# Cross-attention projections through the heads instead of through folded weights, with TensorE in program order

## The chip, the core and the metric

The kernel runs on one core of one Trainium2 chip. The metric is device time in microseconds (us), lower is better. Each engine has its own in-order queue: TensorE (PE, with its weight loads shown as PEld), VectorE (DVE), ScalarE (ACT), GpSimd (POOL), and SyncE (SP), which here only issues transfers. All data are float32.

## The reference

One transformer block on 64 sequences of 32 tokens, width 256. Every sequence has its own context of 257 rows, width 128.

```python
x = x + xattn(layernorm(x), ctx)     # 16 heads of 64: q from x, k and v from ctx (width 128), softmax over 257
x = x + attn(layernorm(x))           # 4 heads of 64 within the 32 tokens, rotary on half of each head
x = x + ffn(layernorm(x))            # 8 experts, top 2 of softmax, silu(a) * b, weighted sum
# xattn:
qh, kh, vh = heads(q @ Wq), heads(kv @ Wk), heads(kv @ Wv)
out = merge(softmax(qh @ kh.T * 64 ** -0.5) @ vh) @ Wo + bo
```

## The kernel before

Keys and values of the cross-attention are never formed. Because the score of head h is `x Wq[h] Wk[h]^T ctx^T`, a setup stage (line 144) multiplies `Wq[h] Wk[h]^T` into `w_qk` (256 x 128 for each head), and likewise `Wv[h] Wo[h]` into `w_vo` (line 158, 128 x 256 for each head). The 257th context row, which does not fit in two blocks of 128, gets a table `u_last` (line 169) that goes to DRAM and comes back by tile (`load_last`). The setup's tiles lie in a pool `raw` that is closed afterwards; a small pool `rope` for the rotary tables comes next.

Tokens are worked in 16 tiles `t` of 128 tokens, that is 4 sequences `b` each. Each (t, b) is one step of the main loop:

- `cross_probs` (L371 to L386): four score matmuls `s` (128 x 257, 32 tokens of 4 heads in the 128 rows). For each, DVE takes the maximum (`nmx`), ACT the exponential and its row sum; then DVE scales all four by the reciprocal sums (`inv`, L380 and L382). It runs one step ahead of its use.
- `probs_transposed` (L394): eight PE transposes `tp` into two banks, copied out to `pt`.
- `cross_mix` (L409): probabilities times context, `pa` (128 x 512), copied by DVE to `cT`.

Two generators fill the loop. `cross_queries(c)` (variable `ahead`) makes the queries of two tiles: layer norm (`normed`, L311 to L319: bn_stats, bn_aggr, a sum on DVE, a power on POOL, a scaling on DVE), transposes `trq`, and for each head two matmuls `pq` (L352) with 256 columns whose results DVE and ACT copy into `q`. `rest(t)` (variable `behind`) does everything that follows for the tile before: `cross_output` (L419, 16 heads into `po`, plus L426 for the last row), then `self_attention` (`trs`, `pqkv`, rotary on DVE, `trqk`, scores `pss`, softmax on DVE and ACT, `pot`, `apo`), then `route` (`trr`, router logits `pr`, running counts `pk`, `pw`, `pb`, and indirect writes of the rows to their expert). The loop takes one piece of each generator at three places of every step. In the attention part only SP's queue keeps the program's order; a scheduler orders PE, DVE, ACT and POOL by readiness in its own model. The pool `ps` gives PSUM banks under the tags `s` (3), `t` (3) and `a` (2).

After the last tile the routed rows go through the experts in 39 blocks (L739 to L790), with PE in program order.

Of the kernel before, what the change touches and what calls it, by code (L numbers as in the profile page):

```python
# [9 lines left out]
FP = mybir.dt.float32  # L10
# [6 lines left out]
P = 128  # L17
# [29 lines left out]
def block_kernel(  # L47
# [6 lines left out]
    xwq_t: bass.AP,  # L54
    xwk_t: bass.AP,
    xwv_t: bass.AP,
# [18 lines left out]
    ctx.enter_context(tc.manual_schedule(engines={SP}))  # L75
    const = ctx.enter_context(tc.tile_pool(name="const", bufs=1))
    ps = ctx.enter_context(tc.tile_pool(name="ps", bufs=3, space=PSUM))

    copies = [0]

    def evacuate(dst, src):
        copies[0] += 1
        if copies[0] % 2:
            nc.vector.tensor_copy(dst, src)
        else:
            nc.scalar.copy(dst, src)  # L86
# [21 lines left out]
    w_qk = const.tile([P, XH, 2, KVD], FP, name="w_qk")  # L108
    w_vo = const.tile([P, XH, D], FP, name="w_vo")
# [11 lines left out]
    setup = ExitStack()  # L121
    raw = setup.enter_context(tc.tile_pool(name="raw", bufs=1))
    xwq_sb = raw.tile([P, XH // 2, D], FP, name="xwq_sb")
    xwk_sb = raw.tile([P, XH // 2, KVD], FP, name="xwk_sb")
    xwv_sb = raw.tile([P, XH // 2, KVD], FP, name="xwv_sb")
    xwo_sb = raw.tile([P, XH // 2, D], FP, name="xwo_sb")
    load(xwq_sb, xwq_t.rearrange("(c p) k -> p c k", p=P))
    load(xwk_sb, xwk_t.rearrange("(c p) k -> p c k", p=P))
    for t in range(2):
        load(xs[t], x[t * P : (t + 1) * P, :])  # L130
    load(xwv_sb, xwv_t.rearrange("(c p) k -> p c k", p=P))
    load(xwo_sb, xwo.rearrange("(c p) k -> p c k", p=P))
    context0 = load_context(0)
    last_sb = const.tile([P, NB], FP, name="last_sb")
    load(last_sb, ctx_last)
    load(xbo_bc, xbo.partition_broadcast(P))

    for h in range(XH):  # L140
        c, r = h // 2, (h % 2) * HD
        pq = ps.tile([P, 2, KVD], FP, tag="s", name=f"pq{h}")
        for k in range(2):
            nc.tensor.matmul(
                pq[:, k, :],
                xwq_sb[r : r + HD, c, k * P : (k + 1) * P],
                xwk_sb[r : r + HD, c, :],
                start=True,
                stop=True,
            )  # L150
        if h % 2:
            nc.vector.tensor_scalar_mul(w_qk[:, h, :, :], pq, QK_SCALE)
        else:
            nc.scalar.mul(w_qk[:, h, :, :], pq, QK_SCALE)
    for h in range(XH):
        c, r = h // 2, (h % 2) * HD
        pv = ps.tile([P, D], FP, tag="t", name=f"pv{h}")
        nc.tensor.matmul(
            pv, xwv_sb[r : r + HD, c, :], xwo_sb[r : r + HD, c, :], start=True, stop=True
        )  # L160
        evacuate(w_vo[:, h, :], pv)


    u_last = tc.dram_tile([4, NB * 4, D], FP, name="u_last")
    u_sb = raw.tile([P, XH // 2, D], FP, name="u_sb")
    for c in range(XH // 2):
        pu = ps.tile([P, D], FP, tag="t", name=f"pu{c}")
        for r in range(2):
            nc.tensor.matmul(
                pu[r * NB : (r + 1) * NB, :], last_sb, w_vo[:, 2 * c + r, :],  # L170
                start=True, stop=True,
            )
        evacuate(u_sb[:, c, :], pu)
    for h4 in range(4):
        r = h4 % 2 * NB
        load(
            u_last[h4].rearrange("(s g) d -> s g d", g=4),
            u_sb[r : r + NB, :, :].rearrange("p (g i) d -> p g i d", i=2)[:, :, h4 // 2, :],
        )
    setup.close()  # L180
# [120 lines left out]
    with attn:  # L301
        qp = attn.enter_context(tc.tile_pool(name="q", bufs=3))
        pp = attn.enter_context(tc.tile_pool(name="p", bufs=3))
        ptp = attn.enter_context(tc.tile_pool(name="pt", bufs=2))
        wk = attn.enter_context(tc.tile_pool(name="wk", bufs=2))
        sm = attn.enter_context(tc.tile_pool(name="sm", bufs=4))

# [14 lines left out]
        def transposed(dst, src, n, name):  # L322

            pt = ps.tile([P, n, P], FP, tag="t", name=f"tr{name}")
            for k in range(n):
                nc.tensor.transpose(pt[:, k, :], src[:, k * P : (k + 1) * P], ident)  # L326
            evacuate(dst, pt)
# [10 lines left out]
        def cross_queries(c):  # L338

            xqT = wk.tile([P, 2, 2 * P], FP, tag="xqT", name=f"xqT{c}")  # L340
            for j in range(2):
                t = 2 * c + j
                xn = normed(t, "q")
                transposed(xqT[:, :, j * P : (j + 1) * P], xn, 2, f"q{t}")
            qs = [qp.tile([P, 4, XH, SEQ], FP, tag="q", name=f"q{2 * c + j}") for j in range(2)]
            for j in range(2):
                queries[2 * c + j] = qs[j]
            yield
            for h in range(XH):
                pq = ps.tile([P, 2 * P], FP, tag="a", bufs=2, name=f"pq{c}_{h}")  # L350
                for k in range(2):
                    nc.tensor.matmul(  # L352
                        pq, w_qk[:, h, k, :], xqT[:, k, :], start=(k == 0), stop=(k == 1)
                    )
                for j in range(2):
                    evacuate(
                        qs[j][:, :, h, :],
                        pq[:, j * P : (j + 1) * P].rearrange("p (b n) -> p b n", n=SEQ),
                    )
                if h % 2:  # L360
                    yield

        def cross_probs(t, b, kvT):


            qb = queries[t][:, b, :, :].rearrange("p h n -> p (h n)")
            sums = sm.tile([P, 4], FP, tag="sums", name=f"sums{t}_{b}")
            pr = pp.tile([P, 4, M], FP, tag="pr", name=f"pr{t}_{b}")
            for g in range(4):
                s = ps.tile([P, M], FP, tag="s", name=f"s{t}_{b}_{g}")  # L370
                nc.tensor.matmul(  # L371
                    s, qb[:, g * P : (g + 1) * P], kvT[:, b, :], start=True, stop=True
                )
                nmx = sm.tile([P, 1], FP, tag="nmx", name=f"nmx{t}_{b}_{g}")
                nc.vector.tensor_reduce(nmx, s, AX.X, ALU.max, negate=True)  # L375
                nc.scalar.activation(  # L376
                    pr[:, g, :], s, AF.Exp, bias=nmx, accum_out=sums[:, g : g + 1]
                )
            inv = sm.tile([P, 4], FP, tag="inv", name=f"inv{t}_{b}")
# [7 lines left out]
            return pr  # L387

        def probs_transposed(t, b, pr, lastT):
            pts = []  # L390
            for j in range(MC):
                tp = ps.tile([P, 4 * P], FP, tag="t", name=f"tp{t}_{b}_{j}")
                for g in range(4):
                    nc.tensor.transpose(  # L394
                        tp[:, g * P : (g + 1) * P], pr[:, g, j * P : (j + 1) * P], ident
                    )
                pt = ptp.tile([P, 4 * P], FP, tag=f"pt{j}", name=f"pt{t}_{b}_{j}")
                if j == 0:
                    nc.vector.tensor_copy(pt, tp)
                else:  # L400
                    nc.scalar.copy(pt, tp)  # L401
                pts.append(pt)
            nc.vector.transpose(lastT[:, b, :], p_last[t % 2][b])
            return pts

        def cross_mix(t, b, pts, kvA, cT):
            pa = ps.tile([P, 4 * P], FP, tag="a", bufs=2, name=f"pa{t}_{b}")
# [6 lines left out]
        def cross_output(t, cT, lastT, ut):  # L414
            xb = wk.tile([P, D], FP, tag="xb", name=f"xb{t}")
            nc.gpsimd.tensor_tensor(xb, xs[t], xbo_bc, ALU.add)
            po = ps.tile([P, D], FP, tag="a", bufs=2, name=f"po{t}")
            for h in range(XH):
                nc.tensor.matmul(  # L419
                    po,  # L420
                    cT[:, h, :, :].rearrange("p b n -> p (b n)"),
                    w_vo[:, h, :],
                    start=(h == 0),
                    stop=False,
                )
            nc.tensor.matmul(  # L426
                po, lastT.rearrange("p b n -> p (b n)"), ut, start=False, stop=True
            )
            nc.vector.tensor_tensor(xs[t], po, xb, ALU.add)

        def self_attention(t):
            xn = normed(t, "s")
# [4 lines left out]
            for lo, hi in ((0, 512), (512, 768)):  # L437
                pq = ps.tile([P, hi - lo], FP, tag="a", bufs=2, name=f"pqkv{t}_{lo}")
# [17 lines left out]
            yield  # L456
            qkT = wk.tile([P, 4, P], FP, tag="qkT", name=f"qkT{t}")
# [6 lines left out]
            for par in range(2):  # L464
                pss = ps.tile([P, 2, SEQ], FP, tag="s", name=f"pss{t}_{par}")
# [30 lines left out]
            pot = ps.tile([P, 2, P], FP, tag="a", bufs=2, name=f"pot{t}")  # L496
# [10 lines left out]
            evacuate(oT, pot)  # L507
# [3 lines left out]
            po = ps.tile([P, D], FP, tag="a", bufs=2, name=f"apo{t}")  # L511
# [4 lines left out]
        def route(t):  # L516


            xr = wk.tile([P, RW], FP, tag="xr", name=f"xr{t}")
            normed(t, "r", xr[:, 0:D])  # L520
# [4 lines left out]
            pr = ps.tile([P, NE], FP, tag="s", name=f"pr{t}")  # L525
# [30 lines left out]
            yield  # L556

            pk = ps.tile([P, NE], FP, tag="s", name=f"pk{t}")
# [17 lines left out]
            pw = ps.tile([NE, P], FP, tag="t", name=f"pw{t}")  # L576
            nc.tensor.transpose(pw, ew, ident)
            ewT = sm.tile([NE, P], FP, tag="rewT", bufs=2, name=f"rewT{t}")
            nc.vector.tensor_copy(ewT, pw)
# [289 lines left out]
```

## Time and profile before

| | |
|---|---|
| three runs | 1050.76 us median (1049.44 to 1054.2) |
| profiled execution | 1047.73 us, span 1046.0 us |
| mean granted TensorE clock in it | 0.946 |
| TensorE busy | 921.9 us, 88% of the span |
| VectorE busy | 582.9 us, 56% |
| ScalarE busy | 304.8 us, 29% |
| first scores; first transposes of probabilities | 53.9 us; 61.2 us |
| `cross_output` of tile 0 begins; of tile 15 begins | 79.5 us; 756.4 us |
| first expert matmul (L763) | 807.2 us |

A line of the profile names the start or the busy time, the engine, the source line, what is written and read, the shape, and in brackets the idle time before it with what ended it. A float32 matmul appears as two instructions (two passes); a transpose as one. An instruction's duration holds its latency, so the rate of a row of matmuls is read from the starts.

### The profile page before, as it was taken

The numbers are of one execution on the slowest core, as the hardware profiler recorded it, in microseconds if no ns is written. First come the engines' busy times: TensorE is split into PE (matmuls) and PEld (weight loads), VectorE is DVE, ScalarE is ACT, GpSimd is POOL, SyncE is SP. The second block draws the span as 40 slices with busy tenths as digits, with TensorE's granted clock in tenths as the row PEclk, the third lists the DMA queues.
The fourth block names the chain that finished last, engine by engine and source line by source line (L and its number), as shares of the span: only waits on it lengthen the run. The fifth ranks groups of instructions, "written<-read, shape, count | busy, mean of one in ns | idle before, by whom it ended". The sixth has DMA issues, their size and how long they took to land. (4 is left out here: it accounts for less than half of the span.)

```text
span 1046.0 us, 15338 instructions
## 1 busy us (share of the span) xinstructions
PE 921.9 (88%) x5272; PEld 713.5 (68%) x5272; DVE 582.9 (56%) x2219; ACT 304.8 (29%) x999; POOL 154.3 (15%) x210
## 2 busy tenths in 40 slices
PE   6599989998999899899989989988863999999992
PEld 5467757675776577577667656756532999999991
DVE  3285775768476666857756685676534333333330
ACT  2262322332232333324223332322200322222220
POOL 3100012011101201100120110011100122222232
PEclk9899998998999999899999999999875999999996
DMA  5600101020101102011110210100003877778722
GB/s 177 201 21 24 39 32 59 1 69 6 54 10 60 59 1 69 6 54 31 39 59 1 69 28 32 54 6 19 16 0 137 283 249 229 233 224 249 207 36 26
DMA packets 39406, 82.82 MB, mean 79 GB/s; under 512 B 5784, under 2 KB 27680, under 8 KB 36256
## 3 DMA queue, kind: packets, MB, share of 16 engines
q1 hardware_dynamic: 32176, 72.38, 20.9%
q0 software_dynamic: 7152, 9.46, 5.0%
q8 instruction: 42, 0.69, 0.3%
q14 instruction: 36, 0.29, 0.1%
HBM read 91.66 MB, written 13.82 MB: 101 GB/s over the span
## 5 line engine op out<-in xcount | busy, mean ns | idle before, releaser
L376 ACT ACTIVATE pr<-s,nmx 128x257 f32<-128x257 f32 x256 | 120.0, 474 | 145.4 <-DVE nmx L375 144.6
L371 PE MATMUL s<-kvT,q 128*128 128x257 f32 x512 | 148.7, 417 | 5.9 <-ACT pr L376 5.1
L352 PE MATMUL pq<-xqT,w_qk 128*128 128x256 f32 x512 | 126.4, 389 | 11.5 <-ACT q L86 11.0
L409 PE MATMUL pa<-pt,kvA 128*128 128x512 f32 x256 | 125.6, 613 | 0.3
L371 PEld LDWEIGHTS s<-kvT,q 128*128 128x128 f32 x512 | 96.4, 203 | 38.2 <-ACT pr L376 14.3
L419 PE MATMUL po<-w_vo,cT 128*128 128x256 f32 x512 | 113.3, 380 | 0.8 <-DVE cT L412 0.8
L352 PEld LDWEIGHTS pq<-xqT,w_qk 128*128 128x128 f32 x512 | 94.0, 193 | 27.4 <-ACT q L86 12.5
L375 DVE TENSOR_REDUCE nmx<-s 128x1 f32<-128x257 f32 x256 | 103.7, 419 | 13.4 <-PE s L371 12.7
L419 PEld LDWEIGHTS po<-w_vo,cT 128*128 128x128 f32 x512 | 97.1, 191 | 15.4 <-DVE cT L412 2.7
L774 DVE SCALAR_TENSOR_TENSOR g<-pb,w1buf,sa 128x128 f32<-128x128 f32 x156 | 44.0, 345 | 107.5 <-PE pb L763 70.0
L790 POOL DMA_INDIRECT out_x<-y,to x39 | 60.6, 1555 | 182.4 <-DMA out_x<-y,to 80.7
L763 PE MATMUL pa<-bxT,w1buf 128*128 128x128 f32 x624 | 77.8, 279 | 4.5 <-DMA w1buf<-in_wall 4.5
L763 PEld LDWEIGHTS pa<-bxT,w1buf 128*128 128x128 f32 x624 | 74.5, 196 | 4.9 <-issue 4.8
L401 ACT COPY pt<-tp 128x512 f32<-128x512 f32 x64 | 37.5, 586 | 136.6 <-PE tp L394 135.1
L763 PE MATMUL pb<-bxT,w1buf 128*128 128x128 f32 x624 | 76.1, 275 | 0.0
L394 PE MATMUL tp<-ident,pr 128*128 128x128 f32 x512 | 75.2, 282 | 0.2
L784 PE MATMUL py<-w2buf,g 128*128 128x256 f32 x312 | 73.8, 380 | 0.8 <-DVE y L789 0.8
L382 DVE TENSOR_SCALAR pr<-pr,inv 128x256 f32<-128x256 f32 x256 | 74.1, 349 | 0.9
L763 PEld LDWEIGHTS pb<-bxT,w1buf 128*128 128x128 f32 x624 | 72.9, 192 | 0.0
L409 PEld LDWEIGHTS pa<-pt,kvA 128*128 128x128 f32 x256 | 45.3, 193 | 40.1 <-issue 23.7
L394 PEld LDWEIGHTS tp<-ident,pr 128*128 128x128 f32 x512 | 62.7, 146 | 9.1 <-issue 3.1
L86 ACT COPY q<-pq 128x128 f32<-128x128 f32 x128 | 33.9, 266 | 103.0 <-PE pq L352 67.1
(196 smaller groups left out, 1085.3 us busy)
## 6 DMA issues: line engine op xcount, KB each, us to landing
w1buf<-in_wall SPq DMA_DIRECT2D x39, 1028.0 KB
w2buf<-in_wall SPq DMA_DIRECT2D x39, 512.0 KB
kvT<-in_ctx_t SPq DMA_DIRECT2D x16, 514.0 KB
kvA<-in_ctx_a SPq DMA_DIRECT2D x16, 512.0 KB
xg<-routed SPq DMA_DIRECT2D x39, 132.5 KB
x<-in_x SPq DMA_DIRECT2D x16, 128.0 KB
out_x<-x SPq DMA_DIRECT2D x16, 128.0 KB
routed<-none SPq DMA_DIRECT2D x8, 132.5 KB
```

Source lines behind the costliest of these rows:

```text
L352: nc.tensor.matmul(pq, w_qk[:, h, k, :], xqT[:, k, :], start=(k == 0), stop=(k == 1))
L371: nc.tensor.matmul(s, qb[:, g * P : (g + 1) * P], kvT[:, b, :], start=True, stop=True)
L375: nc.vector.tensor_reduce(nmx, s, AX.X, ALU.max, negate=True)
L376: nc.scalar.activation(pr[:, g, :], s, AF.Exp, bias=nmx, accum_out=sums[:, g : g + 1])
L382: nc.vector.tensor_scalar(pr[:, g, :ML], pr[:, g, :ML], inv[:, g : g + 1], None, ALU.mult)
L394: nc.tensor.transpose(tp[:, g * P : (g + 1) * P], pr[:, g, j * P : (j + 1) * P], ident)
L409: nc.tensor.matmul(pa, kvA[:, b, j, :], pts[j], start=(j == 0), stop=(j == MC - 1))
L419: nc.tensor.matmul(po, cT[:, h, :, :].rearrange("p b n -> p (b n)"), w_vo[:, h, :], start=(h == 0), stop=False,)
L763: nc.tensor.matmul(dst[:, j, :], w[:, lo : lo + P], xT[:, k, :], start=(k == 0), stop=(k == 1),)
L774: nc.vector.scalar_tensor_tensor(g[:, j, :], pb[:, j, :], w[:, B1 + 4 + j : B1 + 5 + j], sa[:, j, :], ALU.add, ALU.mult,)
L784: nc.tensor.matmul(py, g[:, j, :], w[:, j * D : (j + 1) * D], start=(j == 0), stop=(j == 3),)
L790: nc.gpsimd.indirect_dma_start(out=out[:, :], out_offset=bass.IndirectOffsetOnAxis(ap=to[:, b : b + 1], axis=0), in_=y, in_offset=None, co ...
```

## The change

The folded weights, the setup stage and the pools `raw` go. Queries are made in two steps: `pqh` = x Wq for two heads at a time (K = 128, 128 columns of stationary, 256 moving), scaled by ACT into `qh`; then `of_heads`, which multiplies each head's 64 rows of `qh` with its 64 rows of `Wk`, the even head on rows 0 to 63 of the array and the odd head on rows 64 to 127, into two banks that ACT copies to `q`. The output goes likewise: `pov`, each head's `cT` with 64 columns of `Wv`, even heads to columns 0 to 63 of the array and odd heads to 64 to 127, copied to `ov`, then eight matmuls with `Wo` into `po`. The table of the last row (`last_rows`) is made in the first step of the main loop. TensorE is in program order everywhere. The loop now places single steps: `behind` has six places in each (t, b), the four scores are taken in groups of 2, 1 and 1, and `ahead` starts at an even tile and is spread over two tiles. Empty `yield`s leave places unused. PSUM tags become `s` 3, `t` 2, `a` 3; `p` and `q` pools have two buffers; all `pt` copies and the transposes' copies go to ACT.

```diff
-    ctx.enter_context(tc.manual_schedule(engines={SP}))
+    ctx.enter_context(tc.manual_schedule(engines={SP, mybir.EngineType.PE}))
...
+    for t in range(2):
+        load(xs[t], x[t * P : (t + 1) * P, :])
+    load(xwq_sb, xwq.rearrange("(c p) k -> p c k", p=P))
     load(xwk_sb, xwk_t.rearrange("(c p) k -> p c k", p=P))
+    context0 = load_context(0)
+    load(xwv_sb, xwv)
...
         def cross_queries(c):
             xqT = wk.tile([P, 2, 2 * P], FP, tag="xqT", name=f"xqT{c}")
+            xns = [normed(2 * c + j, "q") for j in range(2)]
+            yield
             for j in range(2):
-                t = 2 * c + j
-                xn = normed(t, "q")
-                transposed(xqT[:, :, j * P : (j + 1) * P], xn, 2, f"q{t}")
...
+                transposed(xqT[:, :, j * P : (j + 1) * P], xns[j], 2, f"q{2 * c + j}")
+            def of_heads(i):
+                pq = [bank([2, 8, SEQ], f"pq{c}_{i}_{par}") for par in range(2)]
+                for mm in range(2):
+                    m = 2 * i + mm
+                    for par in range(2):
+                        r = par * HD
+                        nc.tensor.matmul(
+                            pq[par][:, mm, :, :].rearrange("p b n -> p (b n)"),
+                            xwk_sb[r : r + HD, m, :],
+                            qh[r : r + HD, m, :],
+                            start=True, stop=True,
+                        )
+                for par in range(2):
+                    dst = q[:, :, 4 * i + par : 4 * i + par + 3 : 2, :]
+                    nc.scalar.copy(dst.rearrange("p b h n -> p h b n"), pq[par])
+            for i in range(4):
+                yield
...
+                nc.scalar.mul(qh[:, 2 * i : 2 * i + 2, :], pq, QK_SCALE)
+                if i:
+                    yield
+                    of_heads(i - 1)
+            yield
+            of_heads(3)
...
         def cross_output(t, cT, lastT, ut):
-            for h in range(XH):
-                nc.tensor.matmul(po, cT[:, h, :, :].rearrange("p b n -> p (b n)"), w_vo[:, h, :], start=(h == 0), stop=False)
+            for half in range(2):
+                pv = bank([4, P], f"pov{t}_{half}")
...
+                        nc.tensor.matmul(
+                            pv[par * HD : (par + 1) * HD, i, :],
+                            xwv_sb[:, h * HD : (h + 1) * HD],
+                            cT[:, h, :, :].rearrange("p b n -> p (b n)"),
+                            start=True, stop=True,
+                        )
+                if half:
+                    nc.scalar.copy(ov[:, 4:, :], pv)
+                else:
+                    nc.vector.tensor_copy(ov[:, :4, :], pv)
+                yield
...
             nc.vector.tensor_tensor(xs[t], po, xb, ALU.add)
...
         def rest(t, cT, lastT, ut):
-            cross_output(t, cT, lastT, ut)
-            yield
-            yield from self_attention(t)
-            yield
-            yield from route(t)
+            yield from cross_output(t, cT, lastT, ut)
+            xn = normed(t, "s")
+            yield
+            yield
+            yield from self_attention(t, xn)
+            xr = wk.tile([P, RW], FP, tag="xr", name=f"xr{t}")
+            normed(t, "r", xr[:, 0:D])
+            yield
+            yield
+            yield from route(t, xr)
...
+            probs_transposed(t, b, 0, pr, pts)
             next(behind, None)
+            next(scores, None)
+            next(scores, None)
+            next(behind, None)
+            probs_transposed(t, b, 1, pr, pts)
+            nc.vector.transpose(lastT[:, b, :], p_last[t % 2][b])
+            next(behind, None)
+            next(scores, None)
+            next(behind, None)
+            next(scores, None)
             next(ahead, None)
-            pts = probs_transposed(t, b, now, lastT)
             next(behind, None)
             cross_mix(t, b, pts, kvs[t][1], cT)
             next(behind, None)
-            next(ahead, None)
+            if b % 2 == 0:
+                next(ahead, None)
```

## The prediction

> **What bounds the kernel now.** I read the page's head first.
>
> ```profile
> span 1046.0 us, 15338 instructions
> ...
> PE 921.9 (88%) x5272; PEld 713.5 (68%) x5272; DVE 582.9 (56%) x2219; ACT 304.8 (29%) x999; POOL 154.3 (15%) x210
> ...
> PEclk9899998998999999899999999999875999999996
> ```
>
> TensorE bounds the attention and the experts; only its work and its gaps count. I therefore cut the span by the timeline into A (to 79.5, `cross_output` of tile 0), B (tiles 1 to 15, to 756.4, 676.8 us) and C (the rest, 289.6). The TensorE timeline gives rates from starts.
>
> ```profile
> 24.15 3.67 PE L169 MATMUL pu<-w_vo,last_sb 128*64 128x256 f32 x32
> ...
> 556.03 1.89 PE L352 MATMUL pq<-xqT,w_qk 128*128 128x256 f32 x8
> 557.76 1.04 PE L394 MATMUL tp<-ident,pr 128*128 128x128 f32 x8
> 558.73 0.38 PE L469 MATMUL pss<-qkT 64*32 64x32 f32 x32
> 559.04 1.99 PE L352 MATMUL pq<-xqT,w_qk 128*128 128x256 f32 x8
> ...
> 562.99 0.66 PE L499 MATMUL pot<-diag,qkv 128*64 128x128 f32 x8 [0.15 <-DVE diag L494]
> 563.58 0.70 PE L371 MATMUL s<-kvT,q 128*128 128x257 f32 x2
> ...
> 572.68 0.44 PE L326 MATMUL trr<-ident,xr 128*128 128x128 f32 x2 [0.61 <-DVE xr L319]
> ```
>
> Eight `pq` passes of 256 columns take 557.76 - 556.03 = 1.73 us, 0.216 each; 128 columns cost 0.109. `pu`, on alternating column halves, needs 3.67/32, about 0.11 for 256 columns: halves run two at a time. In the pair of tiles from 495.7 to 585.2 (89.5 us) the passes at these rates make 74.9 us (`po` 14.0, `s` 13.9, `pq` 13.8, `pa` 13.7, `tp` 7.0, the rest 12.5), so 14.6 are gaps. In all of B passes make 550 and gaps 127. About 29 of the gaps (1.9 a tile) belong to small matmuls (`pr`, `pk`, `pw`, `pb`, `pss`, `pot`) and stay. The other 98 are waits and half clock; the table of waits, 62 to 750 us, names them.
>
> ```profile
> PE trr L326 <- DVE xr L319: 18.1, 15, 1.9
> PE trqk L326 <- DVE qkv L455: 13.8, 8, 1.7
> PE trs L326 <- DVE xns L319: 7.1, 8, 1.0
> ```
>
> **Part by part: the start.** The setup matmuls run to 27.7 us; then TensorE waits for ACT, and ACT for a tiny load.
>
> ```profile
> 34.48 1.28 ACT L221 ACT_TABLE_LOAD   x1 [5.66 <-DMA base<-in_freq]
> ...
> 41.91 12.16 PE L352 MATMUL pq<-xqT,w_qk 128*128 128x256 f32 x44 [11.04 <-ACT q L86]
> ```
>
> `base` was issued at 30.9, behind the write of `u_last`, which needs the setup. In the changed order it follows `xbo_bc`, which landed at 15.7 behind the same 4.5 MB. From `sig` to the end of the rotary tables took 5.3 us (35.8 to 41.1), so ACT is free for query copies at about 21.5. Eight copies and two scalings of 512 columns (0.59 each) alternate with TensorE on three banks: 8 us. Table load (1.28) and one softmax bring the first `tp` to an end at 34, not 61. Tile 0 then takes about 11 us for the step that holds `last_rows`, and 6.1, 7.3 and 6.2 for steps with query work (4.32 of `s`, `tp`, `pa`, plus 1.73 for `pqh`, 1.2 for `of_heads`). A ends at 65 instead of 79.5: **-14**.
>
> **B, the work.** Queries of two tiles: 64 passes of 0.216 become 32 full ones and 32 on row halves, 16 times 0.216 if paired: -3.45 a pair of tiles. Output: 32 passes of 0.216 become 32 of 128 columns on column halves (16 times 0.109) and 16 of 0.216: -1.73 a tile. Over B: -27.6 - 25.8 = **-53**. The price of leaving the full array is in the lines above: eight `tp` should have streamed by 558.63 and `pss` starts 0.10 later; `pot`, eight passes two at a time (0.44), leaves the score behind it to 563.58, 0.15 late; and that score's pair takes 0.70, like the group of `pq` behind `pss` 0.10 more than usual, since its first weight load lies open. About 0.3 for one excursion; 30 of them for `pov` and 27 for `of_heads`: **+17**.
>
> The Trainium skill ("TensorEngine Tiling (Array Packing)", Key Properties) says that a change of tiling mode drains the array, without a price; with the drain of about 175 ns that "TensorE: Matmul & The Clock Gate" (Single matmul latency) gives, two drains would be 0.35, an estimate of +20 for this term, and 1064 in the end.
>
> **B, the waits.** Program order removes the scheduler's choice, so each wait is a chain of DVE, ACT and POOL rows less what stands between on TensorE. The chain behind `apo`:
>
> ```profile
> 783.44 0.42 DVE L514 TENSOR_TENSOR x<-apo,axb 128x256 f32<-128x256 f32 x1 [2.17 <-PE apo L513]
> ...
> 784.81 0.55 POOL L316 TENSOR_TENSOR rstdr<-ver,minus_half 128x1 f32<-128x1 f32 x1 [18.87 <-DVE ver L314]
> ...
> 785.86 0.69 PE L326 MATMUL trr<-ident,xr 128*128 128x128 f32 x2 [2.46 <-DVE xr L319]
> ```
>
> From the last pass of `apo` it is 0.44 + 2.42, and one `nmx` (0.42) lies between in DVE's built order: 3.2. Between `apo` and `trr` the new loop has only four `tp` and one score, 0.22 + 0.44 + 0.43 = 1.1. Wait: 2.1, in every tile. In the same way:
> - `trq` of an even tile: three layer norms overlap (one of `rest`, two of `ahead`) with the scalings and a `cT` copy (0.69) between them in DVE's queue; from `xns` on DVE holds three scalings (0.85), `p_last` 0.15, a sum 0.15, bn_stats 0.42, the first `xnq` 0.41, bn_aggr 0.18, `cT` 0.69, a sum 0.15, POOL's power 0.55 and the second `xnq` 0.41, together 4.0, and `trs`, `trq`, `trq` hold only 0.66 of work and stand ahead of `tp` and `pqkv`: 3.6, and 1.2 for `trs` itself (0.1 in odd tiles, where `of_heads` covers it).
> - `trqk`: rotary ends 1.9 after the last `pqkv` pass; two scores and four `tp` cover 1.5: 0.5. `pss` waits for ACT's `qkT`, queued behind two exponentials whose maxima stand behind the rotary: 0.42 + 2 times 0.47 + 0.59 = 2.0, less 0.9 for `trqk` and a score: 1.1.
> - `tp` of the third step: `diag` and the scalings share DVE: 0.3 even, 0.95 odd. `tp` and `pov` at a tile's start: 1.3 even, 0.45 odd. `pk` and `pw` in odd tiles: 1.6. Some 15 exposed weight loads of 0.1: 1.5.
>
> That is 18.4 a pair. Then the clock.
>
> ```profile
> 155.33:158.74 3.41, 1.00 (x5) 0.25 (x3) 2.95 (x15) 0.37 (x1) 1.23 (x3) 1.00 0.00 0
> 158.74:162.15 3.41, 3.41 (x10) 2.63 (x10) 2.28 (x13) 0.91 (x4) 0.55 (x1) 0.50 0.00 0
> ...
> 168.98:172.39 3.41, 3.41 (x15) 1.74 (x14) 1.45 (x5) 1.38 (x6) 0.96 (x1) 1.00 0.39 98
> ```
>
> A stretch of 3.41 us with TensorE busy for 1.00 is followed by half clock (0.50) until one that is full. The three gaps of an even tile's start, 4.8 us with 0.7 of work, must make one such stretch: about 2 us lost in `pqkv`, and 1 more for those that `trr` makes, 3 a pair. The clock gate page (Why this matters for your kernels) wants gaps under about 3 us; each gap here is shorter, so by it alone the term would be 0 and the end 1039. The row shows the rate falling with TensorE still 29% busy, so the row is taken.
>
> Waits and clock: 21.4 a pair, over 7.5 pairs 160, where 98 were: **+62**. B: -53 + 17 + 62 = **+26**. Bounds: 98 if the scheduler's waits merely move (-36 for B), and 1.5 times my sum of 160 (+106). I take the sum; every term is a measured chain, though I step through it by hand.
>
> ACT gains the `pt` and query copies (some 20 us a tile of 47): no bound, but it adds to `pss`. DVE loses 5 us a tile. `p` and `q` with two buffers cost nothing: scores run one step ahead, queries one pair. SP is moved past `u_last`; contexts and x, 1.3 MB, land about 5 us after issue, before the norms read them.
>
> **C.** `pov` and `po` of the last tile: 7.3 becomes 5.9, **-1.4**. Experts are unchanged; `pb` has two banks, each free some 3 us before it is needed, so nothing.
>
> Sum: 1047.7 - 14 + 26 - 1.4 = 1058 for the profiled execution. It lies 3 us below the median of the runs, so the forecast is 1061.
>
> **Rivals.**
> - *Faster: fixed order costs no more than the scheduler's.* Place: the starts of even tiles and `trr`. If gaps without excursions stay at 127, the change gives -14 - 36 - 1.4, that is 1000. For it: in the pair above, the tile with queries has far fewer gaps than the one without (48.7 against 40.8 us with 14 us more work), and `ahead` is now spread over both. Against: `ahead` stands beside `pa`, not in front of `trr`, `trqk` or `pss`. It decides if added waits stay under 40 us, 2.7 a tile.
> - *Row halves do not overlap.* The setup's L144 shows 61 passes in 9.38 us at a cold clock, where one after another would need 13, but only short ones. If 256 columns run singly: +28, 1089.
> - *The start is no earlier,* another load holding ACT: 1075.
>
> **How the numbers follow.** About 0.5% is what a measurement here can tell from none: 1045.5 to 1056. The forecast case has 0.5 with a range of its own from 1037 to 1085 (a tenth of it within 0.5%, plus 0.01 below); the faster rival 0.3 (0.03 of it within 0.5%); halves 0.1; start 0.1. Faster 0.28, same 0.14, slower 0.58. The range 996 to 1090 leaves out a third of the faster rival and the upper half of the second.
>
> **What would show it.** Right: the first `tp` near 34 and tile 0's `pov` near 65; pairs of tiles of 92 to 96 us; a wait of 2 us at every `trr`, three gaps at every even `trs`/`trq`, half clock after them. Wrong: a pair under 88 us, `trq` without a wait, or `of_heads` taking 1.7 us instead of 1.

## The result and the profile after

The changed kernel takes 1064.99 us (median of 12 runs, 1054.73 to 1071.73), the kernel before 1049.35 (12 runs, 1042.82 to 1054.2). The ratio is 1.0138, with a 95% interval of 1.0098 to 1.0179: slower, by about 15 us. The forecast was 1061, range 996 to 1090. For two of the experiments below (e8 and e10) only two runs each are comparable; for these I give the span of the profiled execution and no ratio.

The page's head, for the changed kernel:

```profile
span 1064.6 us, 15731 instructions
...
PE 904.0 (85%) x5448; PEld 667.9 (63%) x5448; DVE 521.3 (49%) x1985; ACT 379.5 (36%) x1070; POOL 154.6 (15%) x210
...
PEclk9799999889998988999898899988685999999996
```

TensorE's busy time fell by 18 us and the span rose by 18.6. Between the third and the 28th slice, which is attention alone, the clock row has ten slices below 9, where the row of before has three. Cut as in the prediction: A, to tile 0's first `pov`, is 74.7 us (79.5 before); B, tiles 1 to 15, 699.1 (676.8); C, the rest, 290.8 (289.6). So the loss is in B.

The table of waits of TensorE between 75 and 773 us names what it waited for, how long in total, how often and at most:

```profile
PE trr L273 <- DVE xr L266: 30.2, 15, 2.0
PE trq L273 <- DVE xnq L266: 17.0, 12, 1.5
PE pss L496 <- ACT qkT L274: 11.7, 15, 0.8
PE trs L273 <- DVE xns L266: 8.4, 8, 1.1
PE pw L605 <- DVE xr L582: 6.5, 9, 0.8
PE trqk L273 <- DVE qkv L481: 5.3, 15, 0.4
```

The counts follow the loop: `trr` waits in all 15 tiles, `trs` in the 7 even ones and in the last, which has no query work left. A wait that hits every time it is due belongs to the written order, not to chance. TensorE's timeline of one even tile shows them in place (start, time, and in brackets the idle time before):

```profile
501.66 1.88 PE L418 MATMUL pa<-pt,kvA 128*128 128x512 f32 x4
504.58 0.41 PE L273 MATMUL trs<-ident,xns 128*128 128x128 f32 x2 [1.04 <-DVE xns L266]
506.49 0.69 PE L273 MATMUL trq<-ident,xnq 128*128 128x128 f32 x2 [1.50 <-DVE xnq L266]
508.45 0.66 PE L273 MATMUL trq<-ident,xnq 128*128 128x128 f32 x2 [1.27 <-DVE xnq L266]
508.91 1.06 PE L408 MATMUL tp<-ident,pr 128*128 128x128 f32 x4
509.76 4.47 PE L466 MATMUL pqkv<-awqkv_sb,xaT 128*128 128x512 f32 x8
...
525.78 0.60 PE L386 MATMUL s<-kvT,q 128*128 128x257 f32 x2
528.40 0.41 PE L273 MATMUL trr<-ident,xr 128*128 128x128 f32 x2 [2.03 <-DVE xr L266]
```

Behind the three gaps four `tp` take 1.06 where 0.60 is usual. The table by windows, cut near the changes of the clock (length, busy time of PE, PEld, DVE, ACT, POOL, clock, DMA share, GB/s), says why:

```profile
502.60:506.10 3.50, 1.35 (x5) 0.31 (x3) 2.70 (x15) 0.66 (x3) 1.94 (x4) 1.00 0.00 0
506.10:509.50 3.40, 1.74 (x7) 1.37 (x8) 1.59 (x6) 0.72 (x2) 0.55 (x1) 0.54 0.00 0
509.50:512.90 3.40, 3.40 (x7) 1.62 (x6) 0.00 (x0) 0.61 (x2) 0.00 (x0) 0.50 0.00 0
512.90:516.30 3.40, 3.02 (x17) 2.28 (x16) 2.86 (x10) 0.67 (x2) 0.00 (x0) 0.95 0.00 0
```

One stretch with TensorE busy for 1.35 of 3.50 us is followed by two at half clock, and the second is full of work that takes twice as long.

### The profile page after: what moved, and what is told of

Same layout as the page of the kernel before. It is cut to its first block, busy times and chain, and to the rows that moved or that the text cites. A ratio compares the mean times of both kernels' runs of the same rounds, so it can differ in the third digit from the quotient of the medians.

```text
span 1064.6 us, 15731 instructions
## 1 busy us (share of the span) xinstructions
PE 904.0 (85%) x5448; PEld 667.9 (63%) x5448; DVE 521.3 (49%) x1985; ACT 379.5 (36%) x1070; POOL 154.6 (15%) x210
## 5 line engine op out<-in xcount | busy, mean ns | idle before, releaser
L418 PE MATMUL pa<-pt,kvA 128*128 128x512 f32 x256 | 133.8, 648 | 0.5
L412 ACT COPY pt<-tp 128x512 f32<-128x512 f32 x128 | 75.1, 587 | 159.9 <-PE tp L408 158.6
L408 PEld LDWEIGHTS tp<-ident,pr 128*128 128x128 f32 x512 | 67.6, 150 | 60.4 <-issue 22.5
L408 PE MATMUL tp<-ident,pr 128*128 128x128 f32 x512 | 97.8, 300 | 5.9 <-DVE pr L399 4.8
L386 PEld LDWEIGHTS s<-kvT,q 128*128 128x128 f32 x512 | 88.8, 194 | 16.2 <-issue 5.9
L807 PEld LDWEIGHTS pb<-bxT,w1buf 128*128 128x128 f32 x624 | 73.1, 193 | 0.0
L363 PE MATMUL pqh<-xqT,xwq_sb 128*128 128x256 f32 x256 | 64.8, 399 | 3.4 <-ACT qh L370 3.0
L814 ACT ACTIVATE sa<-pa,w1buf 128x128 f32<-128x128 f32 x156 | 44.6, 369 | 56.3 <-PE pa L807 56.3
L451 PE MATMUL po<-xwo_sb,ov 128*128 128x256 f32 x256 | 60.3, 379 | 0.0
L828 PEld LDWEIGHTS py<-w2buf,g 128*128 128x128 f32 x312 | 56.4, 190 | 6.1
L598 POOL DMA_INDIRECT routed<-xr,rslots x32 | 32.5, 1015 | 187.3 <-DVE rewT L607 73.3
```

The source lines that it names most:

```text
L363: nc.tensor.matmul(pq[:, mm, :], xwq_sb[:, k, m * P : (m + 1) * P], xqT[:, k, :], start=(k == 0), stop=(k == 1),)
L386: nc.tensor.matmul(s, qb[:, g * P : (g + 1) * P], kvT[:, b, :], start=True, stop=True)
L408: nc.tensor.transpose(tp[:, g * P : (g + 1) * P], pr[:, g, j * P : (j + 1) * P], ident)
L418: nc.tensor.matmul(pa, kvA[:, b, j, :], pts[j], start=(j == 0), stop=(j == MC - 1))
L451: nc.tensor.matmul(po, ov[:, m, :], xwo_sb[:, m, :], start=False, stop=(m == XH // 2 - 1))
L807: nc.tensor.matmul(dst[:, j, :], w[:, lo : lo + P], xT[:, k, :], start=(k == 0), stop=(k == 1),)
```

## The experiments

A, B and C of every profiled execution, in us; "waits" is the idle time of TensorE in B (the trace names a releaser for all but about 2 us of it), "clock" the mean granted in B:

| kernel | median | A | B | C | waits | clock |
|---|---|---|---|---|---|---|
| before | 1049.4 | 79.5 | 676.8 | 289.6 | 55 | 0.967 |
| after | 1065.0 | 74.7 | 699.1 | 290.8 | 89 | 0.934 |
| e1 queries later | 1036.5 | 73.1 | 672.9 | 292.5 | 75 | 0.959 |
| e2 `trr` covered | 1014.4 | 73.2 | 646.4 | 293.7 | 56 | 0.964 |
| e3 both | 995.3 | 72.4 | 627.6 | 295.1 | 48 | 0.989 |
| e4 free order | 957.5 | 69.0 | 597.6 | 291.7 | 28 | 0.989 |
| e5 folded, fixed order | 1108.8 | 96.1 | 714.4 | 297.3 | 90 | 0.959 |
| e6 folded, free order | 1017.8 | 97.8 | 627.5 | 300.3 | 29 | 0.995 |
| e7 `base` first | 1060.2 | 69.8 | 692.8 | 286.9 | 90 | 0.946 |
| e8 e3 unpaired | - | 72.8 | 641.0 | 290.6 | 48 | 0.990 |
| e9 e4, `base` earlier | 950.2 | 62.6 | 596.2 | 287.4 | 29 | 0.993 |
| e10 e4 with e3's moves | - | 65.5 | 584.7 | 290.6 | 24 | 0.997 |
| e11 e4 with all | 939.3 | 62.6 | 586.6 | 297.4 | 23 | 0.991 |
| e12 e3, `pov` whole | 990.2 | 73.2 | 618.3 | 291.5 | 48 | 0.989 |

C scatters by 13 us although its code is nearly the same everywhere, and B by 6 between the changed kernel and e7, whose loops are the same: a few us of a median or of one B are not to be explained.

**e1: queries later.** Theory: the fixed order's places make the waits. Rival: the chains are as long, and the next thing waits.

```diff
         def cross_queries(c):
             xqT = wk.tile([P, 2, 2 * P], FP, tag="xqT", name=f"xqT{c}")
+            yield
             xns = [normed(2 * c + j, "q") for j in range(2)]
```

> Only the place of the next pair's query norms and transposes changes: the norms are issued at the end of an even tile's first sequence, behind the attention's own trs, and trq stands in the second sequence, behind pqkv, trqk and the scores. Theory of the forecast (the fixed order's waits cost it): trs's wait falls from 8.4 us over tiles 1 to 15 to about 1 and trq's from 17.0 to 0, that is -24; the half-clock stretches of 6.83 us that begin at 8 of the even tiles' starts go with them, worth about 1.5 us each: 1065 becomes 1030 to 1042. Rival (the wait moves: the chain is as long and something else is late next): trq or the trqk and pss behind it take up the wait, and the time stays within 8 us of 1065.

Measured: 1036.5 us, 0.9892 of the kernel before (0.9816 to 0.9968). The 17 us of `trq` are gone from B; `trqk` took up 4 of them and the sum of the waits fell by 14, as the table of waits (73 to 746 us) shows:

```profile
PE trr L273 <- DVE xr L266: 30.2, 15, 2.0
PE pss L497 <- ACT qkT L274: 12.3, 15, 1.0
PE trqk L273 <- DVE qkv L482: 9.5, 15, 1.1
PE trs L273 <- DVE xns L266: 8.3, 8, 1.1
```

One expectation missed: `trs` waits as before. The expectation had put its wait in even tiles on the query norms that share DVE with it. In e1 DVE still works the statistics of one of them between (bn_stats at 126.23 in one even tile), but they lengthen nothing: from the start of the sum behind `po` to the start of the scaling it takes 2.6 us there (125.12 to 127.73) and 2.6 us in the last tile, where there is no query norm (711.76 to 714.35). Where query work stands on TensorE between `po` and `trs`, in the odd tiles, there is no wait in either kernel; in the last tile, where there is none, it is 1.04 again. So what is missing is cover; the query norms on DVE are not the cause.

**e2: cover for `trr`.**

```diff
             nc.vector.tensor_scalar(ew, ex, inv, None, ALU.mult)
-            yield
-            yield
+            for _ in range(4):
+                yield
...
             normed(t, "r", xr[:, 0:D])
-            yield
-            yield
+            for _ in range(4):
+                yield
             yield from route(t, xr)
```

> Only the router's steps move: trr stands two steps later, behind a score, query work and the two passes of pa, and pk and pb follow two and four steps later than they did. Theory of the forecast: trr waits 30.2 us over tiles 1 to 15 because 1.1 us of work stands where the chain needs 3.2; with 3.0 to 4.8 us of work there the wait goes, while pr may wait 0.2 a tile for xrT: 1065 becomes 1035 to 1045, with trs and trq waiting as they do now (8.4 and 17.0). Rival (TensorE would be held anyway by the next thing in the chain): pk, pw or pb wait in its place and the time stays above 1055.

Measured: 1014.4 us, 0.9672 (0.9587 to 0.9757), 51 us less than the changed kernel and not 27. The table of waits (73 to 719 us) has no `trr` left:

```profile
PE trq L273 <- DVE xnq L266: 17.5, 12, 1.5
PE pss L496 <- ACT qkT L274: 11.7, 15, 0.8
PE trs L273 <- DVE xns L266: 8.3, 8, 1.1
```

B fell by 52.7. The waits explain 33 of it. The half clock that came with them is another 15: by the starts of the passes, those at half clock lost 34 us against their full rate in the changed kernel and 19 here. The expectation had counted the waits alone.

**e3: both.**

> Both moves together. Theory of the forecast: the two add, since the waits lie in different sequences: -24 and -27, and with no gap longer than about 1 us left the half clock of tiles 1 to 15 goes as well, for which the forecast had put 3 us a pair: 990 to 1012, below the kernel before. Rival (half clock comes by itself, whatever the gaps): the waits go, but the granted clock stays at 0.92 to 0.93, and the time is 1015 to 1025.

Measured: 995.3 us, 0.9501 (0.9441 to 0.9561): 5% below the kernel before, with every matmul of the change in it and TensorE still in program order. The clock in B is 0.989, so half clock did not come by itself: it followed the gaps. The rivals of e1 to e3 fall.

**e4: the same work, order left to the scheduler.**

```diff
-    ctx.enter_context(tc.manual_schedule(engines={SP, mybir.EngineType.PE}))
+    ctx.enter_context(tc.manual_schedule(engines={SP}))
...
+        with tc.manual_schedule(engines={mybir.EngineType.PE}):
             for b in range(-2, NBK + 3):
```

> The projections in two steps with the changed loop, but TensorE's order in the attention left to the scheduler, as in the kernel before; only the experts keep the program's order. Theory of the forecast (the work is 36 us less, the fixed order's waits and clock give 62 back): if the scheduler's gaps are what they were before (127 us in tiles 1 to 15, of which 29 stay) the time is 1000 to 1015. Rival (the gaps come from the finer mixing of modes and steps, not from the order's being fixed): 1050 to 1070, with the same waits at trr and trq.

Measured: 957.5 us, 0.9143 (0.9075 to 0.9211). It is the plainest answer: the changed kernel in the order of a scheduler is 9% faster than the kernel before, and the fixed order as it was written turns that into 1.4% slower. (The 9% are the two steps and the new loop together; e5 and e6 part them.) The theory is right in its direction and 43 us too small. The table of waits (69 to 666 us):

```profile
PE s L386 <- ACT pr L391: 7.5, 30, 0.4
PE trq L273 <- DVE xnq L266: 7.1, 12, 1.0
PE trs L273 <- DVE xns L266: 5.1, 8, 1.2
PE trqk L273 <- DVE qkv L481: 2.6, 7, 0.4
```

How it hides `trr` shows in TensorE's timeline: ten score passes and two `tp`, mostly work of the next sequence, are drawn in between `apo` and `trr`, which starts 4.4 us after `apo` starts and waits for nothing. The two halves of `pov` are put together, 32 passes in one excursion.

```profile
349.27 1.97 PE L434 MATMUL pov<-cT,xwv_sb 128*64 128x128 f32 x32
...
374.86 1.13 PE L542 MATMUL apo<-awo_sb,oT 128*128 128x256 f32 x4
375.83 1.46 PE L386 MATMUL s<-kvT,q 128*128 128x257 f32 x6
377.54 1.42 PE L386 MATMUL s<-kvT,q 128*128 128x257 f32 x4 [0.25 <-ACT pr L391]
378.80 0.38 PE L408 MATMUL tp<-ident,pr 128*128 128x128 f32 x2
379.27 0.44 PE L273 MATMUL trr<-ident,xr 128*128 128x128 f32 x2
```

**e5 and e6: the old work in the new loop,** in program order and in the scheduler's. In place of `pqh` and `of_heads`, 8 steps of two heads; in place of `pov` and `po`, four steps of four heads:

```diff
-                pq = bank([2, 2 * P], f"pqh{c}_{i}")
...
+                            w_qk[:, 2 * i + j, k, :],
...
+            for h in range(XH):
+                nc.tensor.matmul(
+                    po,
+                    cT[:, h, :, :].rearrange("p b n -> p (b n)"),
+                    w_vo[:, h, :],
...
+                if h in (3, 7, 11):
+                    yield
```

> The changed loop in the program's order, with the same places and the same number of steps, but with the folded weights and the setup of the kernel before: 64 full passes for a pair's queries and 32 for a tile's output. Theory of the forecast (two steps are worth 53 us of passes in tiles 1 to 15, less 17 for leaving the full array): +36 in these tiles, or +42 if one excursion costs the 0.19 us that the traces of the first runs show (0.093 going in and 0.093 coming out), and about 10 at the start, where the setup is back: 1065 becomes 1110 to 1118. Rival (the two steps are themselves what makes the waits and the half clock): 1065 or less.

> The same folded weights in the changed loop, with TensorE's order in the attention left to the scheduler. It differs from the kernel before in the finer steps alone, and from e4_free_order (957 us) in the work alone. Theory A (the work is worth 42 in tiles 1 to 15, 10 at the start and 1 at the end, and the finer steps the rest of the 88 us that e4_free_order gained): 957 + 53 = 1010, 35 below the kernel before. Theory B (the finer steps give the scheduler nothing; the two-step work itself has fewer gaps): 1040 to 1050, as the kernel before.

Measured: 1108.8 us (ratio 1.0521, 1.0439 to 1.0602) and 1017.8 (0.9672, 0.9602 to 0.9743). Both totals lie near the forecast's theory, but not by its parts. In e5, A costs 21 more and C, by its scatter, 6.5; B only 15 where +36 was expected. Its waits are those of the changed kernel (90 and 89), its half clock costs 11 less (23 against 34), and I don't know why; some 10 us more of the difference are not accounted for. In the scheduler's order the same difference of work is worth 29.9 in B. The four kernels make a square: fixed against free order is worth 91 us with the folded weights and 108 with the two steps. And e6 against the kernel before, with the same work, has 49 us less in B: the new loop with its finer steps (and its copies on ACT and PSUM banks, which I did not part from them) helps a scheduler by itself, which the prediction had not thought of.

**e7: the start.**

```diff
+    base = const.tile([P, 1], FP, name="base")
+    load(base, freq.partition_broadcast(P))
     for t in range(2):
         load(xs[t], x[t * P : (t + 1) * P, :])
...
-    load(base, freq.partition_broadcast(P))
```

> The changed kernel with one load moved: base is issued first, ahead of x, instead of eleventh. Theory of the forecast (ACT is held by this load until the rotary tables are done, and the queries of tile 0 wait for ACT): cos is done at about 10 instead of 24.7, the first query copy starts at about 17, when its passes are done, the first tp comes at 31 to 33 instead of 39.9, and tile 0's pov at 64 to 67 instead of 74.7: 1065 becomes 1055 to 1058. Rival (the weights' loads, or TensorE and ACT taking turns on three banks under a half clock, hold the start anyway): the first tp at 37 or later, the time within 3 us of the changed kernel's.

Measured: 1060.2 us (10 runs; ratio to the kernel before 1.0088, 1.0047 to 1.0128); A 69.8 instead of 74.7. Half of the expectation, and the intervals of the two ratios overlap, so the gain rests on A of the two traces. The first `tp` came at 36.0, between the two theories. The load does hold ACT: in the changed kernel it is issued at 10.07, behind some 4.6 MB of other loads, and ACT waits. The 4.34 us of its neighbour's issue are not that load's own: in the kernel before the issue of `xbo_bc` took 0.43, three earlier issues took 1.7 to 1.9 each, and SP was done with the same loads at 9.9 as well. SP's issues and ACT's row of the changed kernel:

```profile
5.69 4.34 SPq L95 DMA_DIRECT2D xbo_bc<-in_xbo  x1
10.07 0.43 SPq L95 DMA_DIRECT2D base<-in_freq  x1
```
```profile
18.08 1.28 ACT L165 ACT_TABLE_LOAD   x1 [3.56 <-DMA base<-in_freq]
```

With the load first, ACT has its value at 3.57, but TensorE begins later, since the norms now queue behind the rotary's power on POOL, where theirs start at 13.27 instead of 7.35 (ahead, the row of the changed kernel; behind it, that of e7):

```profile
8.43 1.22 PE L273 MATMUL trq<-ident,xnq 128*128 128x128 f32 x4 [8.43 <-DVE xnq L266]
```
```profile
14.31 1.20 PE L273 MATMUL trq<-ident,xnq 128*128 128x128 f32 x4 [14.31 <-DVE xnq L266]
```

**e8: is it the pairing?** e3 with the loops over head pairs and halves exchanged, in `pov` and `of_heads`:

```diff
-                for i in range(4):
-                    m = 4 * half + i
-                    for par in range(2):
+                for par in range(2):
+                    for i in range(4):
+                        m = 4 * half + i
```

> e3_both (995 us) with one thing changed: the passes on halves of the array are issued one half after the other (four pov passes on the lower columns, then four on the upper; two pq passes on the lower rows, then two on the upper), not in turns. Theory of the forecast (two halves run at the same time only if neighbours in the order lie on different halves): eight pov passes take 0.87 less one overlap, 0.76, instead of 0.44, so +0.65 a tile, and four pq passes 0.65 instead of 0.43, so +1.7 for a pair of tiles: 9.8 + 12 = +22, that is 1012 to 1019. Rival (TensorE overlaps them over a longer stretch of its queue): no change, 995.

Measured: span 1004.3 us against 995.0, B +13.4. Neither theory. `pov`, e3 first and e8 second:

```profile
493.71 1.09 PE L435 MATMUL pov<-cT,xwv_sb 128*64 128x128 f32 x16
```
```profile
504.38 1.58 PE L435 MATMUL pov<-cT,xwv_sb 128*64 128x128 f32 x16
```

Sixteen passes, which my expectation had miscounted as eight, take 0.49 more; 30 groups make 14.7, and `of_heads` did not change at all. By the starts, the passes of the two halves overlap only from the fifth to the twelfth of the sixteen: four passes start alone (0.11 to 0.16 apart), then four pairs (the first pair 0.006 apart), then four alone. The trace doesn't name the half of a pass, but the pattern fits the written order if TensorE starts a pass of the other half up to about four places ahead. In `of_heads`, where four passes of one half stand together, that is enough.

**e12: the price of leaving the full array.**

```diff
-                    for par in range(2):
-                        h = 2 * m + par
...
+                    nc.tensor.matmul(
+                        pv[:, i, :],
+                        xwv_sb[:, m * P : (m + 1) * P],
+                        cT[:, 2 * m, :, :].rearrange("p b n -> p (b n)"),
...
```

> e3_both with pov on the whole array: eight matmuls of 128 columns a tile with two heads' weights side by side, instead of sixteen on alternate column halves; the odd heads' context is left out of the result. The passes stream as long as before (16 times 0.109 = 1.74 a tile), only the two excursions a tile are gone. Forecast's price (0.3 an excursion): tiles 1 to 15 take 9.0 us less than the 627.6 of e3_both. Price seen in the traces since (0.093 going in, 0.093 coming out): 5.6 less. Rival (the 0.093 are something else, such as a weight load that stays open in front of any group): no change. By the drain of about 175 ns of the Trainium skill's page on TensorE: Matmul & The Clock Gate (Single matmul latency), taken twice, an estimate of 10.5 less.

Measured: B 618.3, that is 9.3 less; the forecast's price gave 9.0. The neighbours of `pov` in e3 and, second, in e12:

```profile
494.73 1.13 PE L387 MATMUL s<-kvT,q 128*128 128x257 f32 x4
495.80 1.09 PE L435 MATMUL pov<-cT,xwv_sb 128*64 128x128 f32 x16
496.82 0.66 PE L409 MATMUL tp<-ident,pr 128*128 128x128 f32 x4
497.32 0.60 PE L448 MATMUL po<-u,lastT 128*128 128x256 f32 x2
```
```profile
490.17 1.03 PE L387 MATMUL s<-kvT,q 128*128 128x257 f32 x4
491.04 1.05 PE L433 MATMUL pov<-cT,xwv_sb 128*128 128x128 f32 x8
491.93 0.60 PE L409 MATMUL tp<-ident,pr 128*128 128x128 f32 x4
492.36 0.60 PE L446 MATMUL po<-u,lastT 128*128 128x256 f32 x2
```

From start to start the score group takes 1.07 against 0.87, `pov` 1.02 against 0.89, the `tp` behind it 0.50 against 0.43. With the first `pov` of the tile (1.02 against 0.90) and the `tp` ahead of it (0.59 against 0.49), from the same two timelines, this makes 0.62 a tile, 0.3 an excursion, and 15 tiles of it are the 9.3. (The medians differ by 5 alone, but the two runs of e12 lie 11 apart; B and the timelines carry this reading. e12 also halves the number of weight loads; their share was not parted.) The 0.19 that I had read from the switches alone, after the first runs, left out the first passes inside the group and behind it.

**e9 to e11: towards a better kernel.**

> e4_free_order (957 us) with the load of base moved from behind xbo_bc to behind the first context, so that it lands at about 8 us instead of 18, after the norms of tiles 0 and 1 have passed DVE and POOL. Theory (base held ACT, and with it the query copies; e7_base_first gained less than the forecast because its rotary steps then stood in front of the norms on DVE and POOL, so that trq came at 14.3 instead of 8.4): cos done at about 15, first query copy at 17, tile 0's pov 6 to 8 us earlier than e4_free_order's 69.0: 949 to 952. Rival (the norms still wait for POOL behind the rotary power): trq at 12 or later, pov at 65 or later, 954 to 957.

> e4_free_order with the two moves of e3_both (query norms and transposes later, router's steps later), which the scheduler takes as earlier or later in the program only. Theory (the scheduler had already found the cover: 27.7 us of waits are left in tiles 1 to 15, trq 7 and trs 5 among them): 950 to 957, the gain at most the 7 of trq and some of trs. Rival (the places given in the program matter to the scheduler as much as to the fixed order): 935 to 945.

> All three moves on e4_free_order: base earlier, query norms and transposes later, router's steps later. Theory: the gains add, 943 to 950. Rival (one takes the other's place at the start): as the better of the two alone, 950 to 955.

e9 (`base` loaded behind the first context): 950.2 us, ratio 0.9073 (0.9009 to 0.9136). The load was there for ACT at 12.7, not 8, but `trq` starts at 8.41, A is 62.6, and in A the clock is 1.00 throughout. e10: span 940.8 against e4's 958.4, and B 12.9 less: the rival was right, the places in the program matter to the scheduler too. e11, all three: **939.3 us, 0.8945 of the kernel before (0.8886 to 0.9005)**, the fastest here. That is below the 943 to 950 of its theory: A is that of e9 and B nearly that of e10, so the gains do add; the theory had counted on less from e10. Its page's head:

```profile
PE 853.0 (90%) x5448; PEld 649.0 (69%) x5448; DVE 496.5 (52%) x1985; ACT 370.9 (39%) x1069; POOL 157.4 (17%) x210
...
PEclk9999999999999999999999999997569999999996
```

## Why the prediction was right, and where it was not

- **Work, -53: right.** At the prediction's rates the passes in B add up to 494 us, 55 less than the 549 of the kernel before. The sum had its own slip: -27.6 counts 8 pairs of queries, where B held 7 before and, because `ahead` starts earlier, 6.5 after. The two nearly cancel.
- **Excursions, +17: right for `pov`,** 0.3 each by e12. No run takes those of `of_heads` away; a group of it takes 1.06 where its passes make 0.87, so 0.2 of the 0.3 is seen there. Two drains by the Trainium skill's "TensorE: Matmul & The Clock Gate" (Single matmul latency) had made it 0.35, an estimate; the measured 0.3 decides.
- **Waits and clock, +62: right in sum** (22.3 + 55 - 17 = 60), **not in its split, and in part by luck.** Idle time and half clock together are 89 + 34 = 123 us in B where I had 160, and 55 + 16 = 71 in the kernel before where I had 98: both sides were too high, and their difference came out near. Waits are some 12 a pair; I had 17 without the weight loads. `trr` (2.0; predicted 2.1), `trs` (1.04; 1.2) and `trqk` (0.36; 0.5) fit; `trq` (1.50 and 1.27; together 3.6, where the 4.0 less 0.66 as written give 3.3), `pss` (0.78; 1.1), `pov` and `tp` were too high. The half clock was too low: 34 us in B where I had 22 (3 a pair). I had read that it lasts until one full stretch; the two rows between the second and the third of the prediction's show otherwise:

```profile
162.15:165.57 3.42, 3.42 (x10) 2.53 (x10) 2.16 (x15) 1.66 (x6) 0.00 (x0) 0.50 0.00 0
165.57:168.98 3.41, 3.41 (x14) 2.86 (x13) 2.64 (x9) 1.26 (x4) 1.06 (x1) 0.50 0.13 45
```

  There three full stretches ran at half clock, and in the changed kernel each of the nine spells of half clock between 60 and 700 us lasted two stretches, 6.83 us. e2 shows the same error once more. The skill's "TensorE: Matmul & The Clock Gate" (Why this matters for your kernels), which wants gaps under about 3 us, would have given 0; here the longest gap in B is 2.0 us.
- **Start, -14: the step that failed; it was -4.8.** I had taken the landing of `xbo_bc` in the kernel before, 15.7, for the bound. But ACT had `base`, next in line, at 18.08, and the table load of 1.28 in front of `sig`, which I had left out, waits for `base` too. `cos` was done at 24.7, not 21.5; then half clock, from 25.1 to 32.0 and from 38.8 to 49.0, of which I had counted none: first `tp` at 39.9, and tile 0 took 34.8 us instead of 31. e9, in the scheduler's order, has neither the late load nor the half clock, and its A is 62.6; in program order this was not tried.
- **C, -1.4:** +1.2, inside its scatter.
- **Rivals.** "Fixed order costs no more than the scheduler's" is refuted by e4: as written it costs 108 us more, and with e3's places still 54 (spans of 995.0 and, for e10, 940.8). Its 1000 was also no floor, since I had priced the scheduler by the gaps of before (98 that could go, of 127). In e4 all gaps of B are 104 and in e6, without the new excursions, 85. "Row halves do not overlap" falls: eight passes of `of_heads` take 1.06 us from start to start, where one after another would need 1.73. "The start is no earlier" held to two thirds, as a term, not as a case of its own.

Pairs of tiles with query work took 92.4 to 95.5 us (predicted 92 to 96).

What stays open: why e5's half clock costs less than that of the changed kernel with the same waits, where some 10 us more of its difference went, and what e10's scheduler made of the places that it was given.

## What to carry to other kernels

When an order is fixed by hand, find for each matmul that needs another engine's result the chain from the last pass that feeds it, and count the work that the order puts between; where the work is shorter, the difference is paid in every iteration, and a few empty steps moved (e2: 51 us) are worth more than the 36 us that the matmuls save after their excursions. Price a change of work and a change of order apart, by running one without the other: here the two steps were worth about -6% (e4 against e6, both in the scheduler's order) and the fixed order +11% (the changed kernel against e4). A wait costs more than its length when it leaves a stretch of TensorE mostly idle, because the clock halves for what follows.

## What the runs showed of the hardware

- **The clock goes by stretches of 3.41 us, and by how busy they are.** I cut all 14 traces between 60 and 700 us into the stretches in which the clock changes, and took TensorE's busy share in each that ran at full clock. Busy below 0.40: all 35 were followed by half clock. 0.40 to 0.45: 19 of 20. 0.45 to 0.50: 7 of 19. 0.50 to 0.75: 10 of 189. Above: none of 2232. Back to full clock it went only behind stretches that were at least 0.80 busy, and behind 67 of 90 of those. No single gap decides, and the same gap falls on one stretch or on two: in e1 equal `trr` waits of 2.0 us bring half clock at some tiles and not at others.
- **Halves of the array overlap over a short queue,** about four passes by e8's starts: blocks of four passes (`of_heads`) lost nothing, blocks of eight (`pov`) 0.49 us a group.
- **A load of 512 bytes reached ACT 8 us after its issue began** behind some 4.6 MB of other loads (10.07 to 18.08), and after 2.8 us where it was the first (e7: issued at 0.74, ACT's table load at 3.57).
